# Edge counts moved from layer 0's products to a column of ones in layer 3's row buffers of a graph network kernel

## The chip, the cores and the metric

The kernel runs on one core of one Trainium2 chip. The metric is the device time of one execution in microseconds (us). Nine executions of the kernel before took 10261.73 to 10279.91 us, with a median of 10266.07. A separate execution was recorded by the hardware profiler. In the profile, PE is the matrix engine (PEld its loading of weights), DVE the vector engine, ACT the engine for activations and copies, POOL the general engine that here issues the indirect gathers, and SP the engine that issues the plain DMAs. L with a number is a line of the kernel before.

## The reference

A graph with 12500 nodes, 128 features a node and 212500 edges, sorted by destination, goes through four layers. Each has the form x = x + layer(relu(layernorm(x))), and each sums messages over the edges that end at a node.

```python
# layer 0: attention with 4 heads and edge features
attn = leaky_relu((cat(Wh[src], Wh[dst]) * a).sum(-1)) + edge_feat @ W_e.T
alpha = segment_softmax(attn, dst)
x = x + layer_norm(gelu(segment_sum(alpha * Wh[src], dst)))
# layer 1: messages weighted by an edge weight; layer 2: tensor products
# layer 3: mean over the edges, two products, normalisation over the nodes
agg = segment_sum(h[src], dst)
cnt = segment_sum(ones, dst)
out = agg / maximum(cnt, 1) @ W_l.T + b_l + h @ W_r.T
x = x + (out - mean(out, 0)) * rsqrt(var(out, 0) + eps) * gamma + beta
```

The counts `cnt` depend on the destinations alone and are used in layer 3 only.

## The kernel before, in words

**Tiling.** Nodes are taken in 98 blocks of 128 and, for the work on whole nodes, in 25 node steps of 4 blocks. Edges are taken in 208 groups of 1024, each held as 8 tiles (T) of 128 edges on the 128 partitions. Since edges are sorted by destination, a group's destinations lie in a window of 128 nodes. One-hot tables of destinations (128 edges by 128 nodes) turn the sum over edges into matrix products: the product of a tile's messages with its table adds 128 edges to 128 nodes. Eight products accumulate in PSUM, and DVE adds the result to a slice of the accumulator `acc.t` whose start is read from a table into a register. In layers 0 to 2 the accumulator is a ring of 2048 nodes (RW) and one window, and node steps empty it; in layer 3 it has all nodes, features on the partitions.

**Layer 0** (L1100 to L1146) walks over all 208 groups with a software pipeline whose order is written out by hand (no planner). Iteration g steps a node step if one is due (nodes.step, which works LAG + 2 groups behind the last group of its nodes, LAG = 7), a small part of the index work for later layers (slots.step), loads the edge data of group g + 2, starts the gather of group g's rows into one tile X of 8 tiles by 132 columns (L664, on POOL; the pool holds LAG + 5 = 12 such tiles), transposes edge features on PE (L1003), copies them on ACT (L1005), forms logits on PE (L1007, L1012), builds group g − 6's one-hot table on ACT, and takes steps of the softmax weights. Then `add_up` (L1095, L1097) adds group g − 8's products into `cnt` and `acc.t` on DVE, each behind a register load, and `spread_out` multiplies group g − 7's rows with their weights on DVE (L1083), which frees X, and issues eight fp32 products for the sums (L1087). For the first 121 groups (G0), which cover node blocks 0 to 55, eight more products of a column of ones with the same one-hot tables follow (L1089); they count the edges of each node in the second half of PSUM tile `pag`. After the loop, a DMA writes the counts, `cnt`, to `cnt16` in DRAM.

**Layers 1 and 3** handle blocks 0 to 55 by such groups and the other 42 blocks by *windows*: tables of the edges' source rows already in SBUF (`tabS`) are spread by products (L1455, PSUM tile px), copied to bf16 on ACT (L1466, tiles xb with a column of ones at the end) and summed with one-hot products (L1441, PSUM tile pw, 385 columns), so that windows get their counts as one column. A window has 26 such steps; its one-hot tables are made on DVE (L1403, L1405), the second from `relc`, the relative position of each slot's destination.

**Layer 3** (L1503 to L1558). Its rows are gathered from a table that holds each row as three bf16 parts (384 columns). Iteration g issues the 8 gathers of group g into 8 separate tiles (gather_apart, L672, a pool of 36), builds its one-hot table on DVE (L679), adds group g − 3's transposed sums into `acc.t` (L1534), reduces group g − 2's three parts from PSUM tile `pg` (L1538), issues the eight bf16 products of group g − 1 (L1545) with some ten window steps between them, and transposes group g − 2's sums on PE into `pm` (L1552). `pg` has one buffer. An iteration also takes one step of at most one node step (`node3`); node steps wait in a list. For blocks by groups, a node step loads its counts from `cnt16` by a DMA (L562), spreads them over the partitions by a product (L565), takes the maximum with 1 and the reciprocal on DVE (L568, L569), scales the sums (L571), and goes on with transpositions, the two products, the bias and the statistics (L575 to L586), with a pause (yield) after each stage. Node steps for blocks by windows begin at the transpositions. The loop goes on until groups, windows and node steps are done. `closing` then normalises and writes the output.

Of the kernel before, what the change touches and what calls it, by code (L numbers as in the profile page):

```python
# [92 lines left out]
def gnn_kernel(ctx: ExitStack, tc, x, src, dst, ef16, ef9, ew, W0, We0, a0, lns, lnb, W1, b1,  # L93
# [109 lines left out]
    relc = cst.tile([P, NW, NT], F, name="relc")  # L203
# [3 lines left out]
    bir = tmp.tile([P, NG], I, name="bir")  # L207
# [223 lines left out]
    cnt16 = dram.tile([1, CW], B16, name="cnt16")  # L431
# [123 lines left out]
    def node3(sp, pp, k, tabS, stats):  # L555
# [4 lines left out]
        if b0 < W0_:  # L560
            cn = sp.tile([1, nb * P], B16, name="cn")
            nc.sync.dma_start(cn, cnt16[:, cols(k)])  # L562
            yield
# [103 lines left out]
    def gather_apart(sp, table, idx, bufs):  # L667

        ts = []
        for s in range(T):  # L670
            ts.append(sp.tile([P, table.shape[1]], table.dtype, name="X", bufs=bufs))
            pool.indirect_dma_start(out=ts[-1], out_offset=None, in_=table[:, :],  # L672
                                    in_offset=bass.IndirectOffsetOnAxis(ap=idx[:, s : s + 1], axis=0))
        return ts
# [286 lines left out]
    with (tc.tile_pool(name="e0", bufs=2) as sp, tc.tile_pool(name="e0p", bufs=2, space=PSUM) as pp,  # L961
# [14 lines left out]
        pag = pp.tile([P, 2, W], F, name="pag", bufs=1)  # L976
# [5 lines left out]
        cnt = sp.tile([1, CW], B16, name="cnt", bufs=1)  # L982
        vec.memset(cnt, 0.0)
# [13 lines left out]
        def logits(g):  # L997

            e, rb, sdw = loads.pop(g)
            X = xs[g] = sp.tile([P, T, P + H], F, name="X", bufs=LAG + 5)  # L1000
# [78 lines left out]
        def spread_out(g):  # L1079
# [6 lines left out]
            for t in range(T):  # L1086
                pe.matmul(pag[:, 0, :], msg[:, t, :], S[:, t, :], start=t == 0, stop=t == T - 1)  # L1087
            for t in range(T if g < G0 else 0):
                pe.matmul(pag[:1, 1, :], ones[:, :1], S[:, t, :], start=t == 0, stop=t == T - 1)  # L1089

        def add_up(g):
            p = pag
            if g < G0:
                win = ds(areg.load(bi3[0:1, g : g + 1], BM), W)
                vec.tensor_tensor(cnt[:, win], cnt[:, win], p[:1, 1, :], ALU.add)  # L1095
            win = ds(areg.load(bir[0:1, g : g + 1], RW - 1), W)
            areg.end(vec.tensor_tensor(acc.t[:, win], acc.t[:, win], p[:, 0, :], ALU.add))  # L1097
# [51 lines left out]
        nc.sync.dma_start(cnt16, cnt)  # L1149
# [89 lines left out]
    with (tc.tile_pool(name="t1", bufs=1) as tp, tc.tile_pool(name="e1", bufs=3) as sp,  # L1239
# [16 lines left out]
        with tc.manual_schedule():  # L1256
            g = -1
            while g < G0 + 4 or alive or here or there or waiting:
# [8 lines left out]
                if g < G0:  # L1267
                    X[g] = gather_apart(sp, htab[0], si[:, g, :], 96)
# [223 lines left out]
    with tc.tile_pool(name="l3", bufs=1) as lp:  # L1492
        acc.t, acc.ring = lp.tile([P, AW], F, name="acc3"), None
        stats = lp.tile([P, NK, 6], F, name="stats")
        with (tc.tile_pool(name="t3", bufs=1) as tp, tc.tile_pool(name="e3", bufs=2) as sp,
# [4 lines left out]
            for t in xb:  # L1500
                vec.memset(t[:, 3 * P :], 1.0)
            pm = pp.tile([P, 4, P], F, name="pm")
# [5 lines left out]
            with tc.manual_schedule():  # L1508
# [3 lines left out]
                windows3 = tabled(sp, pp, xb, tabS, pm, stats, waiting.append)  # L1512
                g, count, nk, alive = -1, 0, 0, True
                while g < G0 + 8 or alive or going or waiting:
                    g += 1
                    if g < G0:
                        X[g] = gather_apart(sp, tab3, si[:, g, :], 36)
# [239 lines left out]
```

## Time and profile before

| what | value |
|---|---|
| runs without profile | 10266.07 us median of 9 (10261.73 to 10279.91) |
| profiled execution, its own time | 10299.82 us |
| its span | 10298.1 us, 122470 instructions |
| mean granted clock of PE | 0.718 |
| busy over the span | PE 5784.0 (56%), PEld 4204.7 (41%), DVE 5287.6 (51%), ACT 2832.6 (28%), POOL 5115.7 (50%) |
| bytes moved by DMA | 674.77 MB, mean 66 GB/s |

The stages lie in the span as follows, in us from its start, by the first and last instruction of their lines: setup 0 to 230, layer 0 to 3490, layer 1 to 5345, layer 2 to 8426, layer 3's groups and windows to 10192, the last node steps to 10256 and the closing to 10299.

A row of the profile has a line, an engine, an operation, its output and inputs by the program's names, the tile's form and the number of instructions; behind the bar stand the busy time in us and the mean of one in ns, and then the idle time just before them on that engine, with what ended most of it. "issue" is time in which the engine waited for nothing that the profile shows, and "remote" a wait whose last signal came long after the record of the instruction that gives it. A line of the timeline has the start, the duration, the engine, the line, the operation and, in brackets, the idle time before it.

### The profile page before, as it was taken

The numbers are of one execution on the slowest core, as the hardware profiler recorded it, in microseconds if no ns is written. First come the engines' busy times: TensorE is split into PE (matmuls) and PEld (weight loads), VectorE is DVE, ScalarE is ACT, GpSimd is POOL, SyncE is SP. The second block draws the span as 40 slices with busy tenths as digits, with TensorE's granted clock in tenths as the row PEclk, the third lists the DMA queues.
The fourth block names the chain that finished last, engine by engine and source line by source line (L and its number), as shares of the span: only waits on it lengthen the run. The fifth ranks groups of instructions, "written<-read, shape, count | busy, mean of one in ns | idle before, by whom it ended". The sixth has DMA issues, their size and how long they took to land.

```text
span 10298.1 us, 122470 instructions
## 1 busy us (share of the span) xinstructions
PE 5784.0 (56%) x41651; PEld 4204.7 (41%) x41652; DVE 5287.6 (51%) x10323; ACT 2832.6 (28%) x7693; POOL 5115.7 (50%) x5372
## 2 busy tenths in 40 slices
PE   3245444453333248877774666666666655666666
PEld 2244333343333235555544555655655641111112
DVE  5466565565665424333344666666666652333333
ACT  1132232233332213333331222222222222333333
POOL 0554545555555355555525555555555435555552
PEclk7576666665555568888886777777777776777777
DMA  5232232233333322222211111111111122222223
GB/s 85 62 75 69 69 71 72 71 74 73 75 72 76 72 54 76 70 72 71 73 50 41 49 46 47 47 48 49 47 47 47 46 83 76 76 77 77 76 77 85
DMA packets 741320, 674.77 MB, mean 66 GB/s; under 512 B 341298, under 2 KB 629427, under 8 KB 740660
## 3 DMA queue, kind: packets, MB, share of 16 engines
q0 software_dynamic: 186624, 382.17, 15.2%
q1 hardware_dynamic: 554057, 284.66, 10.8%
q8 instruction: 329, 5.39, 0.2%
q14 instruction: 310, 2.54, 0.1%
HBM read 603.93 MB, written 63.30 MB: 65 GB/s over the span
## 4 chain that ended last, share of the span: by engine, by line


## 5 line engine op out<-in xcount | busy, mean ns | idle before, releaser
L664 POOL DMA_INDIRECT X<-tab,si x1664 | 1615.8, 971 | 1547.0 <-DVE msg L1083 755.3
L664 POOL DMA_INDIRECT X<-htab,si x1664 | 1570.5, 944 | 1376.5 <-ACT A L1319 871.5
L672 POOL DMA_INDIRECT X<-htab,si x968 | 934.5, 965 | 700.0 <-PE pag L1287 310.4
L672 POOL DMA_INDIRECT X<-tab,si x968 | 916.7, 947 | 621.0 <-PE pg L1545 210.3
L1087 PE MATMUL pag<-oh,msg 128*128 128x128 f32 x3328 | 729.2, 408 | 378.0 <-DVE msg L1083 340.5
L1087 PEld LDWEIGHTS pag<-oh,msg 128*128 128x128 f32 x3328 | 676.5, 310 | 393.5 <-DVE msg L1083 345.9
L1466 ACT CAST xb<-px 128x384 bf16<-128x384 f32 x1050 | 495.5, 479 | 1181.6 <-PE px L1455 500.9
L1309 PE MATMUL py<-mixer,eT 72*128 72x120 f32 x416 | 157.9, 481 | 1090.8 <-ACT eT L1308 990.3
L1224 ACT ACTIVATE xs<-px,wslot 128x128 f32<-128x128 f32 x1050 | 373.7, 366 | 1225.9 <-PE px L1212 572.2
L1344 PE MATMUL pag<-oh,A 128*128 128x128 f32 x3328 | 709.6, 403 | 0.0
L1344 PEld LDWEIGHTS pag<-oh,A 128*128 128x128 f32 x3328 | 695.0, 317 | 0.2 <-ACT R L1347 0.2
L1007 PE MATMUL pt<-WeB,eT 128*128 128x32 f32 x416 | 122.0, 384 | 982.1 <-ACT eT L1005 681.0
L1545 PE MATMUL pg<-X,oh 128*128 128x384 bf16 x968 | 399.1, 422 | 444.2 <-DVE f L1538 330.4
L679 DVE TENSOR_TENSOR oh<-iop,rel 128x1024 f32<-128x1024 f32 (+1 forms) x321 | 389.7, 1214 | 501.8 <-remote 307.1
L1287 PE MATMUL pag<-oh,X 128*128 128x128 f32 x1936 | 454.9, 326 | 318.4 <-DVE acc L1280 173.4
L1346 ACT COPY R<-pag 128x256 f32<-128x256 f32 x208 | 77.4, 372 | 1988.3 <-remote 1450.6
L1212 PE MATMUL px<-tabS,oha 128*32 128x128 f32 x8652 | 524.3, 318 | 169.1 <-issue 84.5
L1193 PE MATMUL pw<-ohb,xs 128*128 128x128 f32 x2100 | 587.8, 367 | 11.1 <-ACT xs L1224 6.9
L1309 PEld LDWEIGHTS py<-mixer,eT 72*128 72x128 f32 x416 | 100.9, 302 | 1148.9 <-ACT eT L1308 1042.0
L1455 PE MATMUL px<-tabS,oha 128*32 128x384 bf16 x4326 | 456.6, 409 | 182.5 <-issue 131.2
L1354 DVE TENSOR_TENSOR acc<-acc,po 128x128 f32 x208 | 59.8, 288 | 958.1 <-remote 850.6
L1007 PEld LDWEIGHTS pt<-WeB,eT 128*128 128x128 f32 x416 | 95.0, 284 | 1040.0 <-ACT eT L1005 722.8
(454 smaller groups left out, 12643.5 us busy)
## 6 DMA issues: line engine op xcount, KB each, us to landing
lob<-lo SPq DMA_DIRECT2D x252, 224.0 KB
rb<-rel SPq DMA_DIRECT2D x208, 256.0 KB
X<-tab,si POOLq DMA_INDIRECT x2632
X<-htab,si POOLq DMA_INDIRECT x2632
xtab<-xv SPq DMA_DIRECT2D x72, 256.0 KB
xv<-xtab SPq DMA_DIRECT2D x72, 256.0 KB
lob<-lo SPq DMA_DIRECT2D x84, 160.0 KB
ef<-in_edge_attr_dram SPq DMA_DIRECT2D x51, 256.0 KB
```

Of the source, the lines that this page charges most:

```text
L664: pool.indirect_dma_start(out=t[:, s, :], out_offset=None, in_=table[:, :], in_offset=bass.IndirectOffsetOnAxis(ap=idx[:, s : s + 1], axis=0))
L672: pool.indirect_dma_start(out=ts[-1], out_offset=None, in_=table[:, :], in_offset=bass.IndirectOffsetOnAxis(ap=idx[:, s : s + 1], axis=0))
L679: vec.tensor_tensor(s, iop[:, None, :].to_broadcast([P, T, W]), r[:, :, None].to_broadcast([P, T, W]), ALU.is_equal)
L1087: pe.matmul(pag[:, 0, :], msg[:, t, :], S[:, t, :], start=t == 0, stop=t == T - 1)
L1193: pe.matmul(pw, x, b, start=j == 0, stop=j == NT - 1)
L1212: pe.matmul(px[q * SL : (q + 1) * SL, :], a[:, jj * P + q * SL : jj * P + (q + 1) * SL], tabS[:, blk, :], start=True, stop=True)
L1224: act.activation(x, px, AF.Copy, scale=by)
L1287: pe.matmul(p, r[t], s[:, t, :], start=t == 0, stop=t == T - 1)
L1344: pe.matmul(pag[: TPK[c] * HD, c, :], lhs, S[:, t, :], start=t == 0, stop=t == T - 1)
L1455: pe.matmul(px[q * SL : (q + 1) * SL, :], a[:, jj * P + q * SL : jj * P + (q + 1) * SL], tabS[:, blk, :], start=True, stop=True)
L1466: act.copy(x[:, : 3 * P], px)
L1545: pe.matmul(p, s[:, t, :], r[t], start=t == 0, stop=t == T - 1)
```

## The change

The counting moves from layer 0 to layer 3. In layer 0, the products of ones (L1089), the adds into `cnt` (L1095), the tile `cnt`, its memset and its final DMA are gone, and `pag` has one half. The pool of gathered rows X holds LAG + 8 = 15 groups instead of 12. For the space, `relc` is kept in bf16 rather than fp32; `bir`, the table of window starts in the ring, is kept until the end.

In layer 3, group rows are gathered into 28 fixed tiles `xg` of 385 columns, used in turn, whose last column is set to one at the start; the products have 385 columns, so that the last one holds each node's count in the group. A new copy takes this column from PSUM into column 129 of f3; a new fp32 product with the identity turns it into a row in `pm[:1, 2, :]`; a new add, ahead of that of the sums and with a register load of its own, adds the row into `cnt`, a ring of 2048 nodes and one window in bf16. When a node step is due, its 512 counts are copied out of the ring to a tile `cn` (3 buffers) and cleared (with the ring's overhang added in at each turn of the ring), and the node step goes to the front of the list of waiting node steps. `node3` gets `cn` handed in, and so has no DMA and one pause less.

```diff
@@ -1,5 +1,6 @@
 import math
 from contextlib import ExitStack
+from itertools import cycle
 from types import SimpleNamespace
 
 import numpy as np
@@ -200,11 +201,11 @@
     widx = cst.tile([P, NG], I, name="widx")
     xall = cst.tile([P, NG], I, name="xall")
     rough = cst.tile([P, 1], I, name="rough")
-    relc = cst.tile([P, NW, NT], F, name="relc")
+    relc = cst.tile([P, NW, NT], B16, name="relc")
     early = ExitStack()
     tmp = early.enter_context(tc.tile_pool(name="acp", bufs=1))
     wslot = tmp.tile([P, NW, NT], F, name="wslot")
-    bir = tmp.tile([P, NG], I, name="bir")
+    bir = cst.tile([P, NG], I, name="bir")
     relx = cst.tile([P, GM, T], F, name="relx")
     oversrc = cst.tile([SL, NW], I, name="oversrc")
     begin = cst.tile([P, NW], I, name="begin")
@@ -428,7 +429,6 @@
     alt = dram.tile([TOT, H], F, name="alt")
     tab3 = dram.tile([N, 3 * P], B16, name="tab3")
     lo16 = dram.tile([NW * NT, P], B16, name="lo16")
-    cnt16 = dram.tile([1, CW], B16, name="cnt16")
     htab = [dram.tile([N, P], F, name=f"htab{i}") for i in range(3)]
     xtab = [dram.tile([N, P], F, name=f"xtab{i}") for i in range(3)]
 
@@ -552,15 +552,12 @@
         vec.tensor_tensor(t3[:, :, 2, :], t, t3[:, :, 1, :], ALU.subtract)
         store_rows(tab3, t3.rearrange("p j k d -> p j (k d)"), b0, nb, 3 * D)
 
-    def node3(sp, pp, k, tabS, stats):
+    def node3(sp, pp, k, cn, tabS, stats):
 
         b0, nb = k * NBK, min(NBK, NB - k * NBK)
         n = min(NBK * P, N - b0 * P)
         am = acc.t[:, cols(k)]
         if b0 < W0_:
-            cn = sp.tile([1, nb * P], B16, name="cn")
-            nc.sync.dma_start(cn, cnt16[:, cols(k)])
-            yield
             pc = pp.tile([P, nb * P], F, name="pct")
             pe.matmul(pc, ones16, cn, start=True, stop=True)
             yield
@@ -664,12 +661,12 @@
             pool.indirect_dma_start(out=t[:, s, :], out_offset=None, in_=table[:, :],
                                     in_offset=bass.IndirectOffsetOnAxis(ap=idx[:, s : s + 1], axis=0))
 
-    def gather_apart(sp, table, idx, bufs):
+    def gather_apart(take, table, idx):
 
         ts = []
         for s in range(T):
-            ts.append(sp.tile([P, table.shape[1]], table.dtype, name="X", bufs=bufs))
-            pool.indirect_dma_start(out=ts[-1], out_offset=None, in_=table[:, :],
+            ts.append(take())
+            pool.indirect_dma_start(out=ts[-1][:, : table.shape[1]], out_offset=None, in_=table[:, :],
                                     in_offset=bass.IndirectOffsetOnAxis(ap=idx[:, s : s + 1], axis=0))
         return ts
 
@@ -973,14 +970,12 @@
         le = pp.tile([P, H, L + 1], F, name="le", bufs=1)
         up = sp.tile([P, NL], F, name="up", bufs=1)
         alp = pp.tile([P, 2, SG, T * H], F, name="alp", bufs=1)
-        pag = pp.tile([P, 2, W], F, name="pag", bufs=1)
+        pag = pp.tile([P, W], F, name="pag", bufs=1)
         vec.memset(cut_m[:, :, L:], -LOW)
         vec.memset(cut_s[:, :, L:], 0.0)
         flat = lambda t: t.rearrange("p h k -> p (h k)")
         breg, areg = Window(SP, True), Window(DVE, True)
         loads, xs, alphas, hots = {}, {}, {}, {}
-        cnt = sp.tile([1, CW], B16, name="cnt", bufs=1)
-        vec.memset(cnt, 0.0)
         feats = feature_stream(ef16f, 16, 4, "ef", sp)
 
         def load(g):
@@ -997,7 +992,7 @@
         def logits(g):
 
             e, rb, sdw = loads.pop(g)
-            X = xs[g] = sp.tile([P, T, P + H], F, name="X", bufs=LAG + 5)
+            X = xs[g] = sp.tile([P, T, P + H], F, name="X", bufs=LAG + 8)
             gather(X, tab0, si[:, g, :])
             pt = pp.tile([P, P + T * H + T * 3 * H], F, name="pt")
             pe.transpose(pt[:, :P], e, ident)
@@ -1084,17 +1079,11 @@
                               X[:, :, :P].rearrange("p t (h d) -> p t h d", h=H),
                               ev[:, :, :, None].to_broadcast([P, T, H, HD]), ALU.mult)
             for t in range(T):
-                pe.matmul(pag[:, 0, :], msg[:, t, :], S[:, t, :], start=t == 0, stop=t == T - 1)
-            for t in range(T if g < G0 else 0):
-                pe.matmul(pag[:1, 1, :], ones[:, :1], S[:, t, :], start=t == 0, stop=t == T - 1)
+                pe.matmul(pag, msg[:, t, :], S[:, t, :], start=t == 0, stop=t == T - 1)
 
         def add_up(g):
-            p = pag
-            if g < G0:
-                win = ds(areg.load(bi3[0:1, g : g + 1], BM), W)
-                vec.tensor_tensor(cnt[:, win], cnt[:, win], p[:1, 1, :], ALU.add)
             win = ds(areg.load(bir[0:1, g : g + 1], RW - 1), W)
-            areg.end(vec.tensor_tensor(acc.t[:, win], acc.t[:, win], p[:, 0, :], ALU.add))
+            areg.end(vec.tensor_tensor(acc.t[:, win], acc.t[:, win], pag, ALU.add))
 
         with tc.manual_schedule():
             load(0)
@@ -1146,7 +1135,6 @@
             while nodes.step(NG + LAG + 2):
                 pass
             slots.close()
-        nc.sync.dma_start(cnt16, cnt)
 
 
     def tabled1(sp, pp, tabS, make):
@@ -1265,7 +1253,7 @@
                 here = [w for w in here if next(w, "end") != "end"]
                 there = [w for w in there if next(w, "end") != "end"]
                 if g < G0:
-                    X[g] = gather_apart(sp, htab[0], si[:, g, :], 96)
+                    X[g] = gather_apart(lambda: sp.tile([P, D], F, name="X", bufs=96), htab[0], si[:, g, :])
                     S[g] = one_hot(sp, relx[:, g - G0 + GM, :] if g >= G0 - GM else rel[:, g, :], eww[:, g, :])
                 if g == 0:
                     full = NB - (LR < P)
@@ -1499,6 +1487,13 @@
             xb = [tp.tile([P, 3 * P + 1], B16, name=f"xb{i}") for i in range(4)]
             for t in xb:
                 vec.memset(t[:, 3 * P :], 1.0)
+
+            xg = [tp.tile([P, 3 * P + 1], B16, name=f"xg{i}") for i in range(28)]
+            for t in xg:
+                vec.memset(t[:, 3 * P :], 1.0)
+            rows3 = cycle(xg)
+            cnt = tp.tile([1, RW + W], B16, name="cnt")
+            vec.memset(cnt, 0.0)
             pm = pp.tile([P, 4, P], F, name="pm")
             reg3 = Window(DVE, True)
             X, S, sums, flat3, going = {}, {}, {}, {}, []
@@ -1509,12 +1504,12 @@
                 vec.memset(tabS[:, NB - 1 :, :], 0.0)
                 full = NB - (LR < P)
                 waiting = []
-                windows3 = tabled(sp, pp, xb, tabS, pm, stats, waiting.append)
+                windows3 = tabled(sp, pp, xb, tabS, pm, stats, lambda k: waiting.append((k, None)))
                 g, count, nk, alive = -1, 0, 0, True
                 while g < G0 + 8 or alive or going or waiting:
                     g += 1
                     if g < G0:
-                        X[g] = gather_apart(sp, tab3, si[:, g, :], 36)
+                        X[g] = gather_apart(lambda: next(rows3), tab3, si[:, g, :])
                     if g == 0:
                         for b in range(0, full, 14):
                             n = min(14, full - b)
@@ -1530,15 +1525,19 @@
                         S[g] = one_hot(sp, relx[:, g - G0 + GM, :] if g >= G0 - GM else rel[:, g, :], dt=B16)
                     h = g - 3
                     if 0 <= h < G0:
+                        win = ds(reg3.load(bir[0:1, h : h + 1], RW - 1), W)
+                        reg3.end(vec.tensor_tensor(cnt[:, win], cnt[:, win], pm[:1, 2, :], ALU.add))
                         win = ds(reg3.load(bi3[0:1, h : h + 1]), W)
                         reg3.end(vec.tensor_tensor(acc.t[:, win], acc.t[:, win], pm[:, 1, :], ALU.add))
                     h = g - 2
                     if 0 <= h < G0:
-                        flat3[h] = sp.tile([P, P], F, name="f3")
-                        vec.tensor_reduce(flat3[h], sums.pop(h).rearrange("p (k f) -> p f k", k=3), AX.X, ALU.add)
+                        flat3[h] = sp.tile([P, P + 1], F, name="f3")
+                        p = sums.pop(h)
+                        vec.tensor_reduce(flat3[h][:, :P], p[:, : 3 * P].rearrange("p (k f) -> p f k", k=3), AX.X, ALU.add)
+                        vec.tensor_copy(flat3[h][:, P:], p[:, 3 * P :])
                     h = g - 1
                     if 0 <= h < G0:
-                        p = sums[h] = pp.tile([P, 3 * P], F, name="pg")
+                        p = sums[h] = pp.tile([P, 3 * P + 1], F, name="pg")
                         s, r = S.pop(h), X.pop(h)
                     for t in range(T):
                         if 0 <= h < G0:
@@ -1549,12 +1548,21 @@
                             count += 1
                     h = g - 2
                     if 0 <= h < G0:
-                        pe.transpose(pm[:, 1, :], flat3.pop(h), ident)
+                        f = flat3.pop(h)
+                        pe.transpose(pm[:, 1, :], f[:, :P], ident)
+                        pe.matmul(pm[:1, 2, :], f[:, P:], ident, start=True, stop=True)
                     while nk < len(nodes_at) and nodes_at[nk] <= g:
-                        waiting.append(nk)
+                        c = nk * NBK * P % RW
+                        if nk and c == 0:
+                            vec.tensor_tensor(cnt[:, :W], cnt[:, :W], cnt[:, RW:], ALU.add)
+                            vec.memset(cnt[:, RW:], 0.0)
+                        cn = ns.tile([1, NBK * P], B16, name="cn", bufs=3)
+                        vec.tensor_copy(cn, cnt[:, c : c + NBK * P])
+                        vec.memset(cnt[:, c : c + NBK * P], 0.0)
+                        waiting.insert(0, (nk, cn))
                         nk += 1
                     if not going and waiting:
-                        going = [node3(ns, np_, waiting.pop(0), tabS, stats)]
+                        going = [node3(ns, np_, *waiting.pop(0), tabS, stats)]
                     going = [w for w in going if next(w, "end") != "end"]
         with tc.tile_pool(name="c3", bufs=3) as sp, tc.tile_pool(name="c3p", bufs=3, space=PSUM) as pp:
             closing(sp, pp, stats, 12)
```

## The prediction

> **What bounds the kernel now.** I read four views in this order: busy time in the stretches of the four layers, the list of waits, the timeline at one turn of layers 0 and 3, and one line's starts through layer 0. All times are us from the start of the profiled span.
>
> The table by stretches has, for each, its length, the busy time of PE, PEld, DVE, ACT and POOL with instruction counts, the granted clock, the DMA share and GB/s. The first row shown is layer 0, the last layer 3.
>
> ```profile
> 230.00:3490.00 3260.00, 1377.77 (x9353) 1155.87 (x9354) 1914.18 (x4145) 961.58 (x2573) 1616.32 (x1667) 0.64 0.29 70
> 3490.00:5345.00 1855.00, 1329.07 (x12977) 868.28 (x12977) 663.79 (x1867) 540.22 (x1394) 971.89 (x1011) 0.80 0.28 70
> 5345.00:8426.00 3081.00, 1833.86 (x11953) 1763.72 (x11953) 1948.59 (x2538) 698.78 (x2391) 1570.86 (x1666) 0.74 0.17 46
> 8426.00:10192.00 1766.00, 1101.06 (x6815) 320.27 (x6816) 578.46 (x1005) 552.47 (x1166) 953.04 (x1010) 0.72 0.30 81
> ```
>
> No engine is above 62% in layer 0 (DVE 59%) or layer 3 (PE 62%). Both are bound by a loop of engines waiting for one another. So taking out an instruction does not give its duration back. The waits name the loops; each line is engine, waiting line, what ended the wait, us in total, times, longest. The first three are of layer 0, the rest of layer 3:
>
> ```profile
> ACT eT L1005 <- remote: 940.8, 102, 45.4
> POOL X L664 <- DVE msg L1083: 755.3, 102, 26.1
> PEld pag L1087 <- DVE msg L1083: 345.9, 138, 6.7
> ...
> PEld L1545 <- DVE f L1538: 367.3, 94, 22.8
> DVE oh L679 <- remote: 211.8, 20, 20.9
> POOL X L672 <- PE pg L1545: 210.3, 180, 5.4
> ```
>
> In layer 0 the gathers (L664) wait for row buffers that the message product (L1083) releases, so they run ahead and are not late: eight of 1.25 us (start to start) are 10 us in a turn of about 15. What is slow is PE → ACT (L1003, L1005) → PE (L1007) → DVE. ACT waits 940.8 us in 102 waits for PE's transposition though PE's record has long ended ("remote"): one transposition begins at 1518.45 and its copy on ACT at 1531.56, while gathers run from 1507.6 to 1529.1. A PE result is seen late while gathers issue; I call that held. In layer 3 the loop is the one PSUM buffer of the products (L1545): they wait for the reduction (L1538), which waits for the products before.
>
> **Layer 0: 968 count products and 121 adds go.** Two rows give what is issued:
>
> ```profile
> L1089 PE MATMUL pag<-oh,ones 128*1 128x128 f32 x1936 | 285.9, 306 | 31.2 <-issue 30.9
> L1095 DVE TENSOR_TENSOR cnt<-cnt,pag 1x128 f32 x121 | 33.4, 276 | 377.6 <-remote 299.1 <-PE pag L1089 27.0 <-PE pt L1003 25.4
> ```
>
> That is 285.9/121 = 2.36 us of PE a turn and 33.4/121 = 0.28 of DVE, or 0.59 with the register load behind it (first count add to next add below). If all stood on the path, 2.95 × 121 = 357 us would go; if held signals covered all, nothing. The trace holds its own experiment: groups 0 to 120 have the counts, the rest do not. Starts of the message product in two stretches of the same loop:
>
> ```profile
> 1512.24 0.27 DVE L1095 TENSOR_TENSOR cnt<-cnt,pag 1x128 f32 x1
> 1512.83 0.29 DVE L1097 TENSOR_TENSOR acc<-acc,pag 128x128 f32 x1 [0.32 <-issue]
> ...
> 1173.90:2262.10 1088.20, 84.91 (x70) 0.69 0.30 71
> 2262.10:3300.00 1037.90, 85.01 (x71) 0.59 0.31 74
> ```
>
> The first stretch holds 70 turns, the second 70 and the start of one more (3299.98). So 1088.2/70 = 15.55 us with counts, (3299.98−2262.12)/70 = 14.83 without: 0.72 a turn, a quarter of the 2.95. Sixty turns on each side gave 0.49, 96 against 48 gave 0.83. I take 0.72 × 121 = −87 us (−59 to −100), the ends 0 and −357 being far from what the same loop shows. Counts' memset (3.2 us, ahead of the loop beside gathers) and their final DMA: nothing; layer 1 follows without reading it.
>
> The granted clock is lower where PE has less to do, 0.69 against 0.59, yet the 16 records of L1087 in a turn cost the same: 247.67/70 = 3.54 and 246.43/70 = 3.52 us. The Trainium skill, "TensorE: Matmul & The Clock Gate", section "HAM oscillation — how this bites in real kernels", says that idle gaps of PE above some 3.4 us drop it to half clock, so that the next work starts cold. By that rule less PE work costs time, and the −87 would shrink to about −58 (rival below); by the row it would not, so the trace does not bear it out for this product.
>
> **Layer 0: 15 groups of row buffers for 12.** The first 12 groups of gathers issue without a pause from 232.1 to 351.9, and in that time ACT's copy starts only at 235.4, 240.2 and 321.5; the first message product comes at 400.4, the next gather at 401.9. Three more groups lengthen the burst by 30 us: +30 if all waits for its end, 0 if none. At the other end, the last gather ends at 3391.5 and the eleven products from 3399.2 to 3486.2 come every 7.9 us, against 14.8. Three more turns without gathers save 3 × 6.9 = −21. In between, a deeper run-ahead buys nothing, as DVE waited for gathers (at L1016) 4.6 us in all. Net +30 − 21 = +9; I take +10 (−21 to +35).
>
> **Layer 3, the boundary of the turns.** Around the end of a turn PE ends the products, transposes the row before (L1552), DVE adds (L1534), reduces (L1538), and PE may start again:
>
> ```profile
> 10175.86 0.29 DVE L1534 TENSOR_TENSOR acc<-acc,pm 128x128 f32 x1
> 10176.07 0.55 DVE L1538 TENSOR_REDUCE f<-pg 128x128 f32<-128x384 f32 x1
> ```
>
> Now PE transposes the count column too (fp32, one by 128: 0.31 us, the mean of L1089 and of L1552); DVE adds the counts ahead of the sums (0.28, L1095) with a register load of its own (0.32 idle in the line shown); and behind the reduction a copy of one column, 128x1 (0.15, L1421), stands before the buffer is free. Behind DVE's new wait are queued the accumulating add, the reduction and the windows' one-hot tables (L1403, L1405). All of it on the path: 0.31+0.28+0.32+0.15 = 1.06 × 121 = +128. If the load falls into the wait: 0.74 × 121 = +90. If only a quarter shows, as in layer 0: 0.74/4 × 121 = +22. The products waited for the reduction in 94 of 121 turns, so the boundary counts mostly; where a signal is held, transposition and count come out together and the 0.31 is hidden, leaving 0.43. I take 0.40 × 121 = +48. Nothing below 0: nothing here starts earlier.
>
> **Layer 3, the rest.** (a) 28 memsets of one column at 0.06 and one of 2176 counts (under 2 us) stand on DVE ahead of the memset of L1509, which held the first gather for 67.5 us: +4. (b) Rows in 28 buffers instead of 36: three and a half groups where four and a half were. Rows come late today for 32.0 us in 20 waits; gathers would also issue later. 0 (±10). (c) One column more per product: 385 columns took 407 ns (L1441), 384 took 422 (L1545): 0. (d) At 14 node steps, a copy and a memset of 1x512 on DVE: between 0.15+0.06 and 0.95+0.48 each (L1421, L1412; L1036, L489), 3 to 20 us: +5. (e) Node steps lose their first DMA and its turn, eight turns to seven, and go ahead of the windows' steps. In the tail the direct steps start every 13.7 us with a window step between (L568 at 10192.0 to 10233.0), until 10254.6. By counting turns five direct and five window steps are left after the groups now; then it is some two and seven. With 10 us for the direct pair and 5 for each window, 45 to 60 us for 63.6: −11 (−4 to −20). (f) The table of relative slots in bf16: the same tables took 1213 ns in fp32 and 1216 in bf16 (L679): 0.
>
> **Sum.** −87 + 10 + 48 + 4 + 5 − 11 = −31 us on the profiled execution's 10299.82 (span 10298.1): 10269. That execution lies 33.75 above the median 10266.07 of the runs; the change does not touch what they differ by, so 10235.
>
> **Rivals.**
> - *Held signals cover layer 3's additions.* As in layer 0 a quarter shows, +22 for +48: 10209. For it: 211.8 us of "remote" before the one-hot in layer 3. Against: the loop there is shorter, and only 94 of 121 waits are the reduction's.
> - *Slower: the count step stands whole on the boundary.* Each turn pays the product, the add, its register load and the copy, 1.06 us: +128 for +48, so 10315. It outweighs layer 0 from (48+31)/121 = 0.65 us a turn. For it: the longest waits of L1545 are on exactly this chain (22.8 us). Against: a quarter only showed in layer 0.
> - *The deeper run-ahead helps by −21* (the burst's end not waited for): 10204. Against it: ACT's second and third copies 81 us apart in the burst.
> - *Colder PE.* With fewer products the remaining 16 of a turn would come to half clock: 16 cost 3.78 there (from 1540.8), not 3.54, 0.24 × 121 = 29 us back: 10264. The trace speaks against it (3.52 at the lower clock). It is the page's rule named above.
>
> **How the numbers follow.** ±0.2% is ±20.5 us, about what a measurement of this kernel tells from none. Likeliest case 0.45, its own range 10190 to 10262 (layer 0 −59 to −100, boundary +30 to +75); it gives faster 0.26, same 0.17, slower 0.02. Boundary covered 0.17, all faster. Boundary whole 0.27: slower 0.24, same 0.03. Run-ahead helps 0.08: faster 0.07, same 0.01. Colder PE 0.03: same. Together faster 0.50, same 0.24, slower 0.26. The range takes the covered boundary with −100 in layer 0 (10196) and half of a further gain by buffers and tail, down to 10160, and up to the whole boundary, 10318; some 0.07 lies below it and 0.12 above.
>
> **What the profile after should show.** Starts of L1083's product 14.8 us apart from the first group on, and layer 0 nearer 3180 than 3260 us long; its first at about 430; the last ones, 14 without gathers, at 7.9. In layer 3 a turn of 14.9 for 14.5, with waits of the products on the new copy and of DVE on the count product. The tail behind the last group near 50 us. Wrong if layer 0 keeps its length (the quarter was the clock's or the nodes'), or if layer 3's turn grows by over 0.65 us.

## The result and the profile after

The changed kernel takes 10181.14 us (median of 10 runs, 10158.71 to 10195.64), the kernel before 10271.03 (median of 31): a ratio of 0.9911, 95% interval 0.9901 to 0.992. That is 90 us faster; 31 had been forecast, 10235 us in a range of 10160 to 10318. The profiled execution took 10181.05 us with a span of 10179.1, right at its median, while that of before lay 29 us above its own. So of the 119 us between the two spans some 29 belong to that one execution, and I can't say in which layer they lie.

Where the time went, from the starts of two instructions in both traces: the message product of layer 0 and the reduction of layer 3, in us from the span's start.

| stretch | before | after | change | forecast |
|---|---|---|---|---|
| to the last message product of layer 0 | 3486.2 | 3424.8 | -61 | -77 |
| from there to the first reduction of layer 3 (layers 1, 2 and layer 3's start) | 4957.4 | 4954.3 | -3 | +4 |
| first to last reduction of layer 3 | 1747.0 | 1718.4 | -29 | +53 |
| last reduction to the end | 107.5 | 81.6 | -26 | -11 |

The same table by stretches of the changed kernel (layer 0, layer 3's groups, the tail):

```profile
230.00:3430.00 3200.00, 1112.30 (x7421) 998.66 (x7422) 1880.98 (x4025) 961.18 (x2574) 1615.51 (x1667) 0.58 0.30 71
8358.00:10100.00 1742.00, 1133.64 (x7069) 327.81 (x7070) 645.44 (x1323) 554.82 (x1167) 958.09 (x1010) 0.75 0.31 82
10100.00:10180.00 80.00, 45.50 (x231) 27.91 (x228) 29.30 (x45) 29.70 (x44) 0.21 (x1) 0.71 0.55 162
```

In layer 0, PE is busy for 265 us less (1377.77 to 1112.30), and the layer is 61 us shorter: PE was not the bound. In layer 3 PE and DVE have more to do (DVE 578.46 to 645.44), and its groups got shorter all the same. The waits, layer 0 in the first three lines, then layer 3:

```profile
ACT eT L1000 <- remote: 803.2, 79, 79.5
POOL X L661 <- DVE msg L1078: 670.1, 70, 25.2
PEld pag L1082 <- DVE msg L1078: 282.6, 116, 5.9
...
POOL xg L669 <- PE pg L1544: 420.2, 325, 6.5
PEld L1544 <- DVE f L1537: 379.8, 98, 24.4
DVE oh L676 <- remote: 96.3, 12, 20.1
ACT xb L1454 <- remote: 76.2, 41, 3.5
POOL xo L1401 <- issue: 11.6, 38, 0.3
```

The products now wait for the new copy (L1537) about as long as for the reduction before (379.8 for 367.3 us), so the boundary is still the loop of layer 3. But the held results are fewer: the one-hot's wait fell from 211.8 to 96.3 us, that of the cast to xb (L1454) from 218.4 to 76.2. And POOL, which had waited for a window's products ahead of the window's own gather, as the second of these lines of before shows, no longer does; it waits for its row buffers instead.

```profile
ACT xb L1466 <- remote: 218.4, 65, 10.9
POOL xo L1413 <- PE pw L1441: 211.0, 37, 11.4
```

The boundary itself looks as forecast (timeline of the changed kernel): count product, count add, 0.53 us of DVE idle for the second register load, then the add of the sums.

```profile
10098.56 0.59 PE L1553 MATMUL pm<-ident,f 128*1 128x128 f32 x2
10099.18 0.27 DVE L1529 TENSOR_TENSOR cnt<-cnt,pm 1x128 f32 x1 [0.42 <-PE pm L1553]
10099.98 0.29 DVE L1531 TENSOR_TENSOR acc<-acc,pm 128x128 f32 x1 [0.53 <-DVE cnt L1529]
```

So two questions: does the boundary cost anything, and what shortened layer 3 against it? Theory A: the 28 row buffers. With 36, the rows of a group that POOL had queued behind a waiting window gather went out in one burst, and during bursts PE's results are held; with 28, buffers pace the gathers. Rival B: buffers are nothing, and the new order of work gains. Rival C: the additions cost nothing, because held signals cover them, or the extra product behind the transposition even brings held results out sooner.

### The profile page after: what moved, and what is told of

Same layout as the page of the kernel before. It is cut to its first block, busy times and chain, and to the rows that moved or that the text cites. A ratio compares the mean times of both kernels' runs of the same rounds, so it can differ in the third digit from the quotient of the medians.

```text
span 10179.1 us, 119421 instructions
## 1 busy us (share of the span) xinstructions
PE 5527.6 (54%) x39957; PEld 4041.0 (40%) x39958; DVE 5304.3 (52%) x10506; ACT 2834.6 (28%) x7693; POOL 5129.2 (50%) x5372
## 4 chain that ended last, share of the span: by engine, by line
PE 28%; another core or an unknown queue 20%; issue 7%; DVE 7%; ACT 6%; DVEq 1%; DMA 1%; SPq 0%; POOL 0%; ACTq 0%; POOLq 0%
PE pw L1181 5%; PE px L1200 4%; PE pag L1332 4%; PE px L1443 3%; ACT A L1307 3%; PE pw L1429 3%; PE pag L1275 3%; PE pg L1544 2%; DVE oh L680 1%; ACT R L1334 1%; DVEq L692 1%; PE po L1339 0%; DVE f L1536 0%; PE pag L1082 0%
## 5 line engine op out<-in xcount | busy, mean ns | idle before, releaser
L661 POOL DMA_INDIRECT X<-tab,si x1664 | 1615.0, 971 | 1426.3 <-DVE msg L1078 670.1
L669 POOL DMA_INDIRECT xg<-tab,si x968 | 921.4, 952 | 796.4 <-PE pg L1544 420.2
L1082 PE MATMUL pag<-oh,msg 128*128 128x128 f32 x3328 | 721.8, 405 | 330.7 <-DVE msg L1078 279.6
L1454 ACT CAST xb<-px 128x384 bf16<-128x384 f32 x1050 | 497.4, 479 | 1137.8 <-PE px L1443 587.6
L1082 PEld LDWEIGHTS pag<-oh,msg 128*128 128x128 f32 x3328 | 669.2, 307 | 346.0 <-DVE msg L1078 282.6
L1544 PE MATMUL pg<-xg,oh 128*128 128x385 bf16 x968 | 393.2, 417 | 432.9 <-DVE f L1537 340.4
```

Of the source, the lines that this page charges most:

```text
L661: pool.indirect_dma_start(out=t[:, s, :], out_offset=None, in_=table[:, :], in_offset=bass.IndirectOffsetOnAxis(ap=idx[:, s : s + 1], axis=0))
L669: pool.indirect_dma_start(out=ts[-1][:, : table.shape[1]], out_offset=None, in_=table[:, :], in_offset=bass.IndirectOffsetOnAxis(ap=idx[:, ...
L1082: pe.matmul(pag, msg[:, t, :], S[:, t, :], start=t == 0, stop=t == T - 1)
L1454: act.copy(x[:, : 3 * P], px)
L1544: pe.matmul(p, s[:, t, :], r[t], start=t == 0, stop=t == T - 1)
```

## The experiments

The runs fell on five chips of two kinds. On two of them (one for the late add and its version with two PSUM tiles, one for 28 buffers without layer 0's adds) the kernel before takes 10262 and 10268 us, as in the forecast. On three it takes 7496 to 7501. There, "remote" ends no wait in any trace (the kernel before was traced there only with fewer row buffers); I call these free chips and the others held chips. Why the chips differ was not found. Each comparison is with runs of the kernel before on the same chip, and stretches are read from the traces as in the table above. Each stretch comes from one execution, and executions of one kernel on a held chip lie up to some 40 us apart (10112 to 10154 for the late add), so small differences between stretches are weak there.

**28 row buffers in layer 3 of the kernel before**, twice:

```diff
-                        X[g] = gather_apart(sp, tab3, si[:, g, :], 36)
+                        X[g] = gather_apart(sp, tab3, si[:, g, :], 28)
```

> The kernel before, with layer 3's pool of row buffers at 28 instead of 36 and nothing else changed. In the changed kernel layer 3's groups (first to last reduction) took 1718 us for 1747 before, although a copy, a product and an add were put on the boundary of each turn; the wait of POOL for the window's own gather (211 us before) is gone and the 'remote' waits of ACT and DVE halved. Theory A, the smaller ring paces the gathers and so fewer PE results are held: layer 3's groups shrink here by 30 to 75 us (to 1670 to 1717), the remote waits of the copy and the one-hot halve, and the total is 10195 to 10240. Rival B, the number of buffers is nothing and the gain is in the new order of work: layer 3's groups stay at 1747 +-12, total within 0.15% of before.

> The kernel before with 28 row buffers in layer 3. On a chip without held results: again 0.999 of before, layer 3's groups at 1253. On one with them, theory A (the smaller ring holds fewer PE results): layer 3's groups 30 to 75 us below 1747, remote waits of the copy and the one-hot halved; rival B (buffers are nothing): 1747 +-12.

Both fell on free chips: 0.9991 (0.9981 to 1.0) and 0.9997 (0.9987 to 1.0007) of before, groups 1252.9 and 1249.8 us. Where nothing is held, the number of buffers is worth nothing. That is A's forecast as well as B's, so it settles nothing for held chips.

**28 buffers in layer 1 too** (there 96 before):

> The kernel before with 28 row buffers in layer 3 instead of 36, and 28 instead of 96 in layer 1, whose time is read apart. On a chip with held results: taking the count product and its add off the boundary brought layer 3's groups from 1718 to 1680, so the boundary costs there too, and something else in the change gains about 1747 - 1718 + 38 + 18 (the copy) = 85 us. Theory A (the smaller ring paces the gathers, fewer results are held): groups at 1645 to 1685 here for 1747, the remote waits of copy and one-hot (218 and 212 us) halved. Rival C (the extra product behind the transposition brings held results out, or another part of the change): 1735 to 1760. For layer 1 (groups and windows, 1855 us), theory A lets it shrink by 20 to 80, too; if its gathers are not what holds, +-12. On a chip without held results: layer 3's groups 1250 as before, layer 1 within 10.

A free chip again: 0.9995 (0.9985 to 1.0004); groups of layer 3 1250.2, and 3547.8 us between layers 0 and 3 for 3550.3 and 3543.7 in the two runs above. Whether layer 1 would gain on a held chip stays open.

**28 buffers in layer 3, and layer 0's count products without their adds:**

```diff
-                win = ds(areg.load(bi3[0:1, g : g + 1], BM), W)
-                vec.tensor_tensor(cnt[:, win], cnt[:, win], p[:1, 1, :], ALU.add)
...
-                        X[g] = gather_apart(sp, tab3, si[:, g, :], 36)
+                        X[g] = gather_apart(sp, tab3, si[:, g, :], 28)
```

> Two parts read apart by their layers. Layer 3: the kernel before with 28 row buffers instead of 36, as above; on a chip with held results theory A gives groups at 1645 to 1685 for 1747, rival C 1735 to 1760; without held results 1250. Layer 0: the count products stay, their 121 adds on DVE and the register loads are left out (the counts stay zero, so the means are sums). Groups 20 to 120 took 11.56 us a turn without held results and 10.65 once products and adds are gone. If the products on PE make the 0.91: 11.5 stays. If the add does, ahead of the sums' add and of the message product on DVE: 10.6 to 10.9. The forecast priced both together, 2.36 and 0.59 issued. With held results the periods are 15.5 and 14.9, and the same split is read.

On a held chip: 10137.42 for 10267.93, 0.9869 (0.985 to 0.9887). Layer 3's groups took 1645.5 us for 1747.0, at the edge of A's forecast and far from C's and B's. The waits of layer 3 in this kernel:

```profile
DVE oh L679 <- remote: 109.1, 20, 20.9
ACT xb L1463 <- remote: 94.6, 50, 3.4
...
POOL xo L1410 <- PE pw L1438: 0.3, 1, 0.3
```

With the number alone changed in layer 3, POOL's wait ahead of the window's gather went from 211.0 to 0.3 us and the held waits halved. Counting gathers that start within 1.7 us of the one before as one burst, bursts of 12 or more had 32% of the 996 gathers between layer 3's first and last reduction before, and 8% here and in the changed kernel. Most of the held time lay in them: of the 600 us that ACT and DVE spent in "remote" waits in that stretch before, 339 fell into these bursts, which fill 23% of it; here it is 62 of 268. So what the number of buffers is worth on a held chip is shown, and where the waits lie bears out the bursts as the way; why a burst holds results is not known. The ring's gain is 101 us by the two traces. By the medians it is 130.5 less the 59 by which the two traces differ outside layer 3's groups (53 of them in layer 0), so 71; the difference is the 30 us by which the profiled execution of before was long against the median on this chip. So 71 to 101.

In layer 0, dropping the adds alone brought the last message product from 3486.2 to 3433.0. The time from the first product to that of group 121 fell from 1861.8 to 1828.1 us, 34 of the 82 that the changed kernel gains there (1779.8); the rest, 48, came with the products and the deeper pool, which this does not part. In the turns of groups 20 to 120 it is 15.20 us for 15.51, and 14.91 in the changed kernel.

**The changed kernel without the count work at layer 3's boundary**, twice (counts left out, so means are sums):

```diff
-                        reg3.end(vec.tensor_tensor(cnt[:, win], cnt[:, win], pm[:1, 2, :], ALU.add))
...
-                        vec.tensor_copy(flat3[h][:, P:], p[:, 3 * P :])
...
-                        pe.matmul(pm[:1, 2, :], f[:, P:], ident, start=True, stop=True)
```

> The changed kernel without the count work at the boundary of layer 3's turns: no copy of the count column, no count product, no count add with its register load (the counts are left out, so the means are sums). Forecast's step: the boundary costs 0.40 us a turn, so layer 3's groups go from 1718 to about 1670 and the total from 10181 to about 10133. Rival, the additions are covered: layer 3's groups within 15 us of 1718. Rival C, the extra product behind the transposition brings held results out sooner, so that the additions were a gain: layer 3's groups get longer by 20 us or more.

> The changed kernel without the count's copy, product and add at the boundary of layer 3's turns (counts left out, means are sums). Without held results it took 1254 us for the groups where the changed kernels with 12 tiles or with the other node order took 1319 and 1298, so the boundary's work cost 0.4 to 0.5 us a turn, as forecast: this is to repeat against the changed kernel itself. With held results, theory A says that the boundary still costs and the ring gains more than it: groups at 1650 to 1690 for 1718; rival C (the boundary's work is covered by held results): 1718 +-12.

Free chips: 0.9816 (0.9798 to 0.9833) and 0.9823 (0.9807 to 0.9839) of before, where the changed kernel is at 0.99. The groups took 1254.5 and 1250.3 us, just what the kernel before with 28 buffers took there (1249.8). Beside the changed kernel's 1312.5 on the chip of the second run (the next experiment), the boundary's work costs 62 us, 0.51 a turn.

**The changed kernel itself on such a chip, and with 20 row buffers:**

> The changed kernel as it is. The four runs before this one were on a chip on which the kernel before takes 7500 us, not 10270, and no wait in its trace ends long after the instruction that releases it. If this call is on such a chip: 7425 to 7432, that is 0.990 of before, with layer 0's last message product at 2488, layer 3's groups at 1300 to 1320 and the tail at 82. On a chip with held results, as in the forecast's profile: 10181, with 3425, 1718 and 82.

> The changed kernel with 20 row buffers in layer 3, two and a half groups. Without held results: rows come later, groups longer by 5 to 40 us. With held results, theory A: fewer are held, groups shorter than 1718 by 10 to 40 us; rival B: not shorter, since 20 buffers only make rows late.

7429.15 for 7496.03, 0.990 (0.9879 to 0.9921): layer 0's last message product at 2486.8 for 2588.0, groups 1312.5 for 1249.8, tail 82.0 for 106.2. (The kernel before has no trace on such a chip; its version with 28 buffers, 0.9997 of it, stands for it here.) So here the change is -101 in layer 0, +63 at the boundary, -24 in the tail. The total ratio is that of the held chip, made of other parts. With 20 buffers 0.9905, groups 1307.7: rows did not come later, against the expectation (the products waited 29.3 us for rows, 29.1 with 28 buffers).

**Twelve groups of row buffers in layer 0, and node steps at the end of the list:**

```diff
-            X = xs[g] = sp.tile([P, T, P + H], F, name="X", bufs=LAG + 8)
+            X = xs[g] = sp.tile([P, T, P + H], F, name="X", bufs=LAG + 5)
```

```diff
-                        waiting.insert(0, (nk, cn))
+                        waiting.append((nk, cn))
```

> The changed kernel with 12 groups of row buffers in layer 0 instead of 15. Forecast's step: three groups fewer give back 30 us at the start (first message product at 400 for 430.6) and cost 21 at the end, so layer 0's last message product comes at 3416 for 3424.8 and the total falls by some 10 us. Then removing the counts alone is worth 70 us in layer 0 (3486.2 to 3416). Rival, the depth of the run-ahead has a price or a gain of its own in the middle: the product's period in groups 20 to 190 differs from that with 15 by over 0.15 us.

> The changed kernel with layer 3's due node steps put at the end of the waiting list, as before, instead of at its front. From the last reduction to the end it took 81.5 us in the changed kernel and 107.5 before. If the order alone makes this gain: 100 to 108 here, total up by about 20. If the missing DMA and pause of the node step make it: 80 to 88. The forecast had 11 us from both together.

Free chip, 0.9901 and 0.9904. With 12 groups the last message product came at 2486.5, with 15 at 2486.8 to 2489.9, and the first at 307 to 310 in all: on a free chip the three more groups are worth nothing either way. With the steps at the end, the tail took 95.9 us (for 82.0 and, before, 106.2): 14 of the tail's gain are the order's, 10 that of the missing DMA and pause. But the groups were 1298.1 for 1312.5 and 1318.8: what the order takes from the tail it puts into the groups, and the total is the same.

**The count add behind the reduction, and two PSUM tiles for the products:**

```diff
-                        win = ds(reg3.load(bir[0:1, h : h + 1], RW - 1), W)
-                        reg3.end(vec.tensor_tensor(cnt[:, win], cnt[:, win], pm[:1, 2, :], ALU.add))
                         win = ds(reg3.load(bi3[0:1, h : h + 1]), W)
...
                         vec.tensor_copy(flat3[h][:, P:], p[:, 3 * P :])
+                    h = g - 3
+                    if 0 <= h < G0:
+                        win = ds(reg3.load(bir[0:1, h : h + 1], RW - 1), W)
+                        reg3.end(vec.tensor_tensor(cnt[:, win], cnt[:, win], pm[:1, 2, :], ALU.add))
```

and for the second, on top of it:

```diff
-        po = pp.tile([P, nb * P], F, name="pn")
+        po = pp.tile([P, nb * P], F, name="pct")
...
-                        p = sums[h] = pp.tile([P, 3 * P + 1], F, name="pg")
+                        p = sums[h] = pp.tile([P, 3 * P + 1], F, name="pg", bufs=2)
```

> The changed kernel with the count add behind the reduction and the copy, so that on the way from the last product of a turn to the first of the next stand neither the count product nor its add, but only the copy (0.15 us). On a chip without held results the three together cost 62 us (1312.5 against 1250.3 for the groups). If they cost by standing on the boundary: 0.15 x 121 = 18 of them stay, groups at 1265 to 1280, total 0.984 to 0.986 of before. Rival, they cost as work of PE and DVE wherever they stand: groups stay at 1300 to 1320, 0.990 of before. On a chip with held results: within 15 us of the changed kernel by the theory that the additions are covered there.

> As the kernel with the late add, and the products of layer 3's groups in two PSUM tiles in turn instead of one (the node step's output shares the tile of its transpositions for it), so that the next products needn't wait for the reduction and the copy of the last. If the boundary is what bounds layer 3's groups: the waits of the products for the copy (231 us) go, groups at 1120 to 1230, total 0.965 to 0.98 of before, then with ACT's cast and PE's own order of work as the next limits. Rival, the windows bound them (the cast waits for their products 724 us): groups above 1250.

Both on a held chip. The late add: 10136.34 for 10261.67, 0.9871 (0.985 to 0.9891), groups 1680.5 for the changed kernel's 1718.4. So count product and add did cost 38 us there by standing on the boundary, 0.31 a turn: they are not covered by held signals, and rival C falls. The medians say the same: the interval of this ratio lies wholly below that of the changed kernel, 0.9901 to 0.992. The boundary in this kernel, with the sums' add right ahead of the reduction and the count add behind the copy:

```profile
9006.98 0.28 DVE L1529 TENSOR_TENSOR acc<-acc,pm 128x128 f32 x1
9007.18 0.55 DVE L1534 TENSOR_REDUCE f<-pg 128x128 f32<-128x384 f32 x1
9007.64 0.15 DVE L1535 COPY f<-pg 128x1 f32<-128x1 f32 x1
9007.71 0.27 DVE L1539 TENSOR_TENSOR cnt<-cnt,pm 1x128 f32 x1
9007.85 0.10 PEld L1546 LDWEIGHTS <-oh 128*128 128x128 bf16 x1 [1.50 <-DVE f L1535]
```

The two tiles: 10039.75, 0.9779 (0.9763 to 0.9796), a version that beats both kernels. Groups 1561.8; the wait of the products for the reduction or the copy, 380 us in the changed kernel, is no longer among their waits, and what is left of them is small:

```profile
PEld L1546 <- issue: 76.2, 178, 2.6
PE pg L1546 <- DMA xg<-tab,si: 35.5, 25, 17.2
PEld L1546 <- DVE oh L676: 17.4, 1, 17.4
```

The tail took 108.0 us for 82.0. Nine node steps are left behind the last reduction in both kernels, but here they end every 6.7 us instead of every 2.8. Each one's transpositions (L572) now wait until ACT has read the step before out of the tile that they share with it (L581), and the granted clock in this stretch is 0.50 for 0.92: one record of the product L578 took 1.06 us (median) for 0.59. So the trace puts the loss down to the shared tile of the node steps, not to the second tile for `pg`; why the clock is lower was not tested. That waiting for the one PSUM tile cost layer 3 some 119 us is shown by this; had the windows alone been the bound, the groups would have stayed at 1680. What bounds the 1561.8 us that are left was not tested, and the expectation's 1120 to 1230 us, worked out from waits on a free chip, was not reached here; on a free chip this kernel has not run.

## Why the prediction was right, and where it was not

The direction and the range held; the size was 31 for 90. It came out by a sum in which one step was wrong by 70 to 100 us, and two others (layer 3's boundary, 25 us more than forecast, and the fifteen groups, 10 more) partly paid for it. Without the ring's gain the parts come to some -18 us on the traces, near the -31 of the sum and within the 20 us that the prediction itself calls hard to tell from nothing. That the direction came out so clearly on this chip is luck: it is owed to a term that had been put at nothing. A turn of layer 3 took 14.3 us for 14.6 where 14.9 for 14.5 had been forecast, for the same reason.

- **Row buffers of layer 3, step (b), "28 buffers instead of 36: 0 (±10)": wrong, the largest error.** They are worth -71 to -101 us on held chips. The prediction had both halves in front of it (held results during bursts in layer 0, and POOL's wait for the window's gather in layer 3), but asked of the ring only whether rows would come late, never whether fewer of them would hold PE's results less.
- **Layer 3's boundary, +48: right in mechanism, too small.** Between the kernel before with 28 buffers (1645.5) and the changed one (1718.4) lie 73 us, or 0.60 a turn for 0.40: 38 for product and add (with the second register load, whose idle is 40.2 us in the two lines below, not all of it on the path), 35 for the rest. In that rest is the copy (17.8 us busy); what else is in it was not parted. On free chips the boundary's three instructions cost 62, and without them the groups were as short as before (1250.3 for 1249.8), so the node steps' copies and memsets and the wider product showed no price there. The rival that took it as covered (+22) is out; the slower rival's 1.06 a turn was not reached.

```profile
DVE acc L1531 <- issue: 26.5, 60, 0.9
DVE acc L1531 <- DVE cnt L1529: 13.7, 32, 0.6
```

- **Layer 0's counts, -87: right.** From the first message product to that of group 121 the changed kernel took 82 us less; in the two later executions on a held chip, which have the same layer 0, 94 and 85 against the one trace of before. The kernel's own comparison of groups with and without counts was the right price. On free chips it was 0.91 a turn (11.56 to 10.65), a little more than the same comparison gives there (11.56 to 10.80 in the groups without counts).
- **Fifteen groups, +10: right in the start, too good at the end.** The first message product came at 430.6 us as forecast (+30). The last 14 took 154.0 us for 161.6, -8 where -21 had been forecast, so the net is +20 (30 - 8, and 2 less in the turns between). Even the 8 is doubtful: with 12 groups and no adds, the last 14 took 134.6 us, less than with 15. Twelve groups without any count work were not run on a held chip, so what the three more are worth there rests on these starts.
- **The tail, -11: right in sign, too small.** It was -26. The steps left over were counted right (two direct and seven by windows), but those by windows came every 2.8 us, not at the 5 that the sum took. By the free chip's two orders 14 of the gain are the order's, but those are paid for in the groups.
- **Layer 3's start +4, bf16, the wider product: nothing seen** (-3 for all of layers 1, 2 and the start). The table in bf16 cost nothing: the line that reads it (L1405, now L1393) has a median of 1084 ns in both. The rows of L679 by which the prediction expected this differ in the type of the output, so they did not show it.
- **Colder PE: no such loss showed, but not for the reason given.** The granted clock in layer 0 fell from 0.64 to 0.58, and the products of L1087, now L1082, took 721.8 us for 729.2. This does not speak against the rule in the Trainium skill, "TensorE: Matmul & The Clock Gate", section "HAM oscillation — how this bites in real kernels", by which idle gaps of PE make the next products cold. The trace agrees with it: the 16 records of a turn took 2.05 us at their fastest, in turns before which PE had been idle for less than 1.7 us, and 3.39 to 3.79 us in each of the 40 turns, in either kernel, before which it had been idle for 3.4 us or more. But with shorter gaps most turns were slow too. In the kernel before 84% of all turns already took 3.4 us or more (78% in the changed one), so there was little left to lose. The 3.54 and 3.52 us that the prediction compared are means over turns of both kinds and can't test the rule.

On the traces the parts add up: -82 + 20 in layer 0 with rounding, -101 + 73 in layer 3, -26 and -3, together -119. What was not tried: 36 buffers in the changed kernel, 20 on a held chip, and the kernel before with 28 buffers and nothing else changed on a held chip (there it ran with layer 0's adds left out).

## What to carry to other kernels

Where a profile has a stage with and a stage without the work that is to go, the difference of their turns is a better price than the instructions' own time: 0.72 us a turn for 2.95 issued, and 0.68 measured. A smaller buffer ring is not only a risk of late data: ask also what the run-ahead disturbs, and look at every wait that stands in the gather queue ahead of the rows. And work that is moved to "an engine with room" is paid for if it lands between the last product of a turn and the first of the next, here with 0.60 us a turn of the 1.06 it takes by itself; a second PSUM tile there was worth more (-97 us by the medians, on top of the late add) than the whole change.

## What the runs showed of the hardware that I had not expected

The same kernel takes 7496 to 7501 us on three chips and 10262 to 10268 on two others. On the first kind layer 0's copy waits for its transposition without any held time, and these lines of the kernel before with 28 buffers (layer 0) show POOL limited by its own issue:

```profile
ACT eT L1005 <- PE pt L1003: 510.1, 134, 15.6
POOL X L664 <- issue: 453.5, 1488, 0.3
```

The first message product comes at 308 us there and at 400 on the held chips, behind the burst of the first 12 groups. Durations of single instructions agree on both kinds (the gather's issue 0.94 to 0.99 us, the cast of 384 columns 0.479); the turn of layer 0 without counts is 10.8 and 14.9 us. Layer 3's groups take 1250 us there in the kernel before with 28 buffers, which is their 996 gathers at 1.25 us; POOL never stood idle for more than 0.3 us between two of them, so POOL bounds this stretch. The 62 us of the boundary's work are thus what it adds above POOL's pace, and the number of buffers can't shorten it. 99% of layer 3's gathers come in bursts of 12 or more there, and no result is held; so a burst alone does not hold results. What holds PE's signals on the other chips while gathers issue is not known from these runs.
